# A two-hop graph layer and an adjacency-ranked layer in one kernel: row-end products merged, x and the adjacency laid out anew in memory

## The chip, the cores and the metric

One Trainium2 chip, of which the program uses one core. The metric is the device time of one execution in microseconds, as the median of several runs. Lower is better.

## The reference, cut to what matters

N is 4096 nodes, D is 64 features. `adj` is 4096 x 4096, float32, with about 0.8% non-zeros and a full diagonal.

```
h = relu(layernorm(x))
for k in range(2):                         # layer 0, two hops
    agg = adj @ h
    h = tanh(concat([agg, h]) @ W[k])      # W[k] is 128 x 64
x = x + h
h = relu(layernorm(x))                     # layer 1
support = h @ weight
mask = (adj != 0)
rank = cumsum(mask, axis=1)
deg = rank[:, -1:]
k = min(deg, 100)
pos = rank - (deg - k)
w = mask * where(pos > 0, 0.5 ** (k - pos), 0)
x = x + (w @ support + bias)
```

So the adjacency is needed as numbers twice (two hops), and once as an ordered mask, from which the weights of layer 1 come as powers of two.

## The kernel before, in words

The adjacency is transposed on the host, so that a block is 128 source nodes (on the partitions) by a chunk of 1024 destination nodes. There are 4 chunks ("rows", index I) of 32 blocks; a block is 512 KB.

Sweep 1 reads every block of every row once, two blocks (a "pair", 1 MB) to a load (L396), 64 pairs in all, as far ahead as there is space. A place is either one of three pair-sized slots of `ring`, or a stretch of `codes` that is not yet needed. For each pair, DVE (and for some pairs ACT, L227 and L228) makes the mask and running counts (`count_pair`, L236 to L248), and PE multiplies the features `h` with the block into `acc`. Blocks of nodes whose x1 (the result of hop one) is known already are "fused": the weights hold h and x1 side by side, 128 columns (L438, one matmul of 0.86 us for 512 columns). Others use 64 columns, two matmuls side by side on the halves of the array (L254, 0.43 us each as a pair goes).

At the end of a row comes `finish_row` (L306), a generator of which one step runs after each pair of the following row, so that PE's work lies between the pairs. ACT copies the sums S and, from row 1 on, F out of PSUM; `totals` (L284) makes the total counts; PE forms `po` and ACT takes its tanh as x1 (transposed); PE turns x1 to node layout with the identity (`nodes`, L208, line L212) and forms in `po1` what the known part gives to hop two (L323, L329, and for row 0 L344, with G summed from blocks that were held); ACT copies both out. Then `set_after` (L293) gets, by products with `tri` and `neg`, how many entries lie behind each half of the blocks, in two rounds (v = 1, 0), and `settle` (L366) subtracts that from the codes.

Sweep 2 reads again, one block (512 KB) to a load (L832), the 72 blocks that hop two still lacks: first those of chunks 3 and 2, then 1, then 0. It has six slots of `ring`, four from block 24 on. `finish_last` (L473) is the row end of row 3 and runs between the first blocks. When a chunk's sum is complete, `finish_x2` (L511) finishes x2: it adds the stored part by a product with the identity (L518), multiplies the sum (L531), takes tanh, adds the input x (loaded again as `xres`, L525), and makes LayerNorm and a split into three bf16 parts. That makes the chunk ready for layer 1.

Layer 1 goes by 64 units of two blocks by a destination chunk. A unit's codes are turned to bf16 weights by ACT (L642, L649) or DVE (L624 to L638), PE multiplies them with the high parts (L692) and then the low part (L704), and when a group of four units ends, the sums are taken out of PSUM (L722 to L741). `finish_out` (L746) multiplies with the layer's weight and adds the residual. The units run between sweep 2's blocks; the last 28 or 30 after them.

The order of all of sweep 2 is written by a planner inside the kernel: `use(engine, us, after)` keeps an estimated clock for each engine, `space` says from when a buffer is free, and `run_chain`, `decode` and `fill` place the next step by these clocks. So an edit of a step's estimated duration, or of when a buffer is given to `space`, moves the order of instructions on PE, ACT and DVE. All loads are issued by SP, in program order: an SP instruction that waits for a buffer holds back all loads behind it.

Of the kernel before, what the change touches and what calls it, by code (L numbers as in the profile page):

```python
# [36 lines left out]
def gnn_kernel(  # L37
# [20 lines left out]

    nc = tc.nc

    N, D = x.shape
# [46 lines left out]
    xv = x.rearrange("(p b) d -> p b d", b=NB)  # L108
# [14 lines left out]
    def load_x(engine, b0, b1):  # L123
        engine.dma_start(pre1[:, b0:b1, :], xv[:, b0:b1, :])
# [7 lines left out]

    def load_weights():
        for h in range(2):
            rows = slice(h * D, (h + 1) * D)
            nc.sync.dma_start(wz[rows, h], Wd)
            nc.sync.dma_start(wa[rows], weight)
            nc.gpsimd.tensor_copy(wh[rows, h], wa[rows])

# [10 lines left out]
    ident = cpool.tile([P, P], F32, name="ident")  # L150
# [4 lines left out]
    neg = cpool.tile([P, P], BF16, name="neg")  # L155
    nc.vector.tensor_scalar(neg, diff, 0.0, -1.0, op0=ALU.is_equal, op1=ALU.mult)

    off = cpool.tile([P, 2], F32, name="off")
    for h in range(2):
        nc.vector.tensor_scalar(  # L160
            off[:, h : h + 1], diff[:, P - 1 : P], float(2 * FULL), float((1 - h) * FULL),
            op0=ALU.mult, op1=ALU.add,
        )
# [43 lines left out]

    def nodes(src):  # L208

        pt = one(name="pt")  # L210
        for t in range(TC):
            nc.tensor.matmul(  # L212
                pt[:, t * P : (t + 1) * P], by_t(src)[:, t // 2, t % 2, :], ident,
                start=True, stop=True, skip_group_check=True,
            )
        return pt.rearrange("p (t c e) -> p t c e", t=TC, c=NC)
# [67 lines left out]
    def totals(I):  # L284

        both = tmp([P, CW], U8, name="both")
        nc.vector.tensor_tensor(both.bitcast(U16), cnts[I % 2][0], cnts[I % 2][1], op=ALU.add)  # L287
        tot = [tmp([P, CW], BF16, name="tot") for _ in range(2)]
        nc.scalar.copy(tot[0], both)  # L289
        nc.scalar.copy(tot[1], cnts[I % 2][1].bitcast(U8))  # L290
        return tot

    def set_after(I, v, tot, banks):  # L293

        for c, pb in enumerate(banks):
            nc.tensor.matmul(  # L296
                pb, tri if v else neg, tot[1 - v][:, c * C : (c + 1) * C],
                start=v == 1, stop=True, skip_group_check=True,
            )
        for c, pb in enumerate(banks):  # L300
            nc.vector.tensor_scalar(  # L301
                after[:, v, I * CW + c * C : I * CW + (c + 1) * C], pb,
                off[:, v : v + 1], float(K), op0=ALU.add, op1=ALU.min,
            )

    def finish_row(I, acc, held):  # L306
        S = tmp(name="S")
        nc.scalar.copy(S, acc[:, NC, :])
        if I:
            F = [tmp(name="F") for _ in range(NC)]  # L310
            for c in range(NC):
                nc.scalar.copy(F[c], acc[:, c, :])
        tot = totals(I)
        yield
        po = one(name="po")
        terms = [(lambda c: wz[:, c, 0, 0], lambda c: S)]
        if I:
            terms.append((lambda c: wz[:, 0, 0, 0], lambda c: F[c]))
        x1T = x1_of(po, I, terms)
        po1 = two(name="po1")  # L320
        if I:
            for c in range(NC):
                nc.tensor.matmul(  # L323
                    po1[c * D : (c + 1) * D, :], wz[:, 1, 1, 0], F[c], start=True, stop=False
                )
        yield
        pt = nodes(x1T)
        for c in range(NC):
            nc.tensor.matmul(  # L329
                po1[c * D : (c + 1) * D, :], wz[:, c, 1, 1], x1T, start=I == 0, stop=I > 0  # L330
            )
        nc.scalar.copy(as_nodes(hx[:, chunk(I), D:]), pt)
        yield
        if I == 0:

            own = [v for k in sorted(held) for v in held[k]]
            for n, (b, a) in enumerate(own):
                agg_pair(acc[:, 0, :], hx[:, b, D:], a, n == 0, n == len(own) - 1)
            held.clear()
            G = tmp(name="G")  # L340
            nc.scalar.copy(G, acc[:, 0, :])
            yield
            for c in range(NC):
                nc.tensor.matmul(  # L344
                    po1[c * D : (c + 1) * D, :], wz[:, c, 1, 0], G, start=False, stop=True
                )
        nc.scalar.copy(flat(pre1[:, chunk(I), :]), po1)
        yield
        banks = [one(name="pb"), two(name="pb")]
        for v in (1, 0):  # L350
            set_after(I, v, tot, banks)
            yield
        all_settle(I)
# [16 lines left out]
    def sweep1():  # L370
        b0 = NB - 2
        load_x(nc.sync, b0, NB)
        load_x(nc.sync, NB - CB, b0)
# [5 lines left out]
        def load(upto, done):  # L379

            while len(tiles) < min(upto, len(pairs)):
# [10 lines left out]
                if k == 0:  # L392
                    for r in range(2):
                        nc.sync.dma_start(a[:, r, :], adjA[I, n + r])
                else:
                    nc.sync.dma_start(a, adjA[I, n : n + 2].rearrange("r p i -> p r i"))  # L396
# [3 lines left out]
        for k, (I, b) in enumerate(pairs):  # L400
# [3 lines left out]
            if k == 0:  # L404
                load(1, 0)
                load_x(nc.sync, NB - 2 * CB, NB - CB)
                load(2, 0)
                load_x(nc.sync, 0, NB - 2 * CB)
# [54 lines left out]
        return acc, totals(I)  # L463
# [9 lines left out]
    def finish_last(acc, tot):  # L473

        I = NCH - 1
        S = tmp(name="S")
# [4 lines left out]
        use("ACT", 1.7, 0.2)  # L481
# [7 lines left out]
        pt = nodes(x1T)  # L489
        nc.scalar.copy(as_nodes(hx[:, chunk(I), D:]), pt)  # L490
        use("ACT", 0.6, use("PE", 1.3) + 0.2)
        po1 = two(name="po1")
        for c in range(NC):
            nc.tensor.matmul(
                po1[c * D : (c + 1) * D, :], wz[:, 1, 1, 0], F[c], start=True, stop=False
            )
        for c in range(NC):
            nc.tensor.matmul(
                po1[c * D : (c + 1) * D, :], wz[:, c, 1, 1], x1T, start=False, stop=True
            )  # L500
        nc.scalar.copy(flat(pre1[:, chunk(I), :]), po1)
        use("ACT", 0.6, use("PE", 1.9) + 0.2)
        yield
        banks = [one(name="pb"), two(name="pb")]
        for v in (1, 0):
            set_after(I, v, tot, banks)
            use("DVE", 1.4, use("PE", 0.5) + 0.2)
            yield
        all_settle(I)

    def finish_x2(I, acc):  # L511

        h = chunk(I)

        pt = one(name="py")
        v = by_t(flat(pre1[:, h, :]))
        for t in range(TC):
            nc.tensor.matmul(  # L518
                pt[:, t * P : (t + 1) * P], v[:, t // 2, t % 2, :], ident,
                start=t == 0, stop=False, skip_group_check=True,  # L520
            )
# [3 lines left out]
        nc.sync.dma_start(xres, xv[:, h, :])  # L525
        t0 = use("ACT", 0.6, clock["PE"] + 0.2)
        use("PE", 1.25)
        yield t0 + 0.1
        v = by_t(S)
        for t in range(TC):  # L530
# [3 lines left out]
                start=False, stop=True, skip_group_check=True,  # L534
            )
        y = tmp(name="y")
        nc.scalar.activation(y, pt, AF.Tanh)
        yield use("ACT", 0.65, use("PE", 1.25) + 0.2) - 0.5
        nc.vector.tensor_tensor(
            as_nodes(pre1[:, h, :]), as_nodes(xres), y.rearrange("p (t c e) -> p t c e", t=TC, c=NC),  # L540
            op=ALU.add,
        )
        t = use("DVE", 0.7, clock["ACT"] + 0.1)
# [132 lines left out]
    def layer1(n):  # L676
# [20 lines left out]
        use("PE", 0.2)  # L697
        for i, acc in zip(todo, accs):
# [10 lines left out]
        for i, acc in zip(todo, accs):  # L709
# [12 lines left out]
            if g not in parted:  # L722
                parted.add(g)
                for q, p in enumerate(part(g)):
                    (nc.vector.tensor_copy if q == 1 else nc.scalar.copy)(p, acc[:, q, :])
                    use("DVE" if q == 1 else "ACT", 0.65, t)
            elif J:
                for q, p in enumerate(part(g)):
                    nc.vector.tensor_tensor(p, acc[:, q, :], p, op=ALU.add)
                    use("DVE", 0.65, t)  # L730
            else:
                ys = part(g)
                for q, p in enumerate(ys):
                    nc.vector.tensor_tensor(p, acc[:, q, :], p, op=ALU.add)
                t = use("DVE", 1.9, t)
# [7 lines left out]

    outs = []

    def finish_out(g, ys):  # L746
        last = g == order[0][-1]
        pt = (one if g % 2 else two)(name="pto")
# [3 lines left out]
        for ks in [range(K4)] if not last else [range(K4 // 2), range(K4 // 2, K4)]:  # L752
            for k in ks:
                cols = slice(k * P, (k + 1) * P)
                for c in range(NC):
                    nc.tensor.matmul(  # L756
                        pt[:, k * P + c * D : k * P + (c + 1) * D], ys[c][:, cols], wa,
                        start=k == c == 0, stop=not last, skip_group_check=True,
# [12 lines left out]
    def sweep2(acc, tot):  # L771
# [7 lines left out]
        space(quad(mbuf.rearrange("p a r i -> p (a r i)").bitcast(I16)))  # L779
# [5 lines left out]
        last = finish_last(acc, tot)  # L785
# [33 lines left out]
        for n in range(0, total, 2):  # L819
# [8 lines left out]
            for r in range(2):  # L828
# [3 lines left out]
                nc.sync.dma_start(a, adjA[I, NB - 1 - b - r])  # L832
# [45 lines left out]
    sweep2(*sweep1())  # L878
# [26 lines left out]
```

## Time and profile before

| what | us |
|---|---|
| median of 3 runs | 392.31 (390.9 to 392.37) |
| the profiled execution | 390.78 |
| its span | 389.0 |
| PE busy | 365.5 (94%) |
| DVE busy | 301.4 (77%) |
| ACT busy | 166.2 (43%) |
| sweep 1's last product ends on PE | 205.5 |
| last adjacency block of sweep 2 used | 333.3 |

Busy time of PE is the time with at least one matmul in flight; matmuls are pipelined, so the mean duration of one (0.6 us for L254) is longer than what it adds to the row. What a matmul costs when they follow closely is read from the chain: four matmuls of L254 with their weight loads ("x8") take 1.72 us there. PE was granted its full clock but for a stretch near 14 to 21 us.

The loads move 108.5 MB. All are made of packets of at most 4 KB: in the trace's packet records 25,728 of 4096 bytes (median 159 ns), 1024 of 2048 bytes (81 ns at the fastest), and a few smaller. At full use the core gets some 410 GB/s.

### The profile page before, as it was taken

Reading aid. Unit: us, or ns where it says so; the run is one execution under the profiler, and the core shown is the slowest. Engines: PE = TensorE matmul, PEld = TensorE weight load, DVE = VectorE, ACT = ScalarE, POOL = GpSimd, SP = SyncE. Lnnn points to the kernel's source line nnn. Section 1 sums busy time; section 2 is a strip of 40 time slices with the busy share of each in tenths; the row PEclk is TensorE's granted clock in tenths of the full one; section 3 lists DMA queues with packets and bytes.
Section 4 is the critical chain, followed back from the end, with each engine's and each line's share of the span. In section 5 each row is a group of like instructions: output and inputs, shape, how many; then the busy total and the mean of one; then the engine's idle time right before and its main releaser. Section 6 shows DMA issues by size and latency. Waiting matters only on the chain.

```text
span 389.0 us, 4496 instructions
## 1 busy us (share of the span) xinstructions
PE 365.5 (94%) x1654; PEld 144.5 (37%) x1668; DVE 301.4 (77%) x565; ACT 166.2 (43%) x164; POOL 22.7 (6%) x21
## 2 busy tenths in 40 slices
PE   3698789999999999999999988999999999999995
PEld 0142223234333443444443323333343333434554
DVE  5979989499989999699889697777846844389943
ACT  2179980754363433410004111744246945388200
POOL 2202100000000000000000030300003000030000
PEclk9699999999999999999999999999999999999999
DMA  7999999999997896578999799588876887000011
GB/s 229 415 411 406 365 408 407 409 408 409 410 345 270 313 327 235 205 291 305 293 350 317 250 417 401 182 283 305 304 265 224 313 312 258 2 2 2 0 56 54
DMA packets 30150, 108.50 MB, mean 279 GB/s; under 512 B 2736, under 2 KB 3376, under 8 KB 30128
## 3 DMA queue, kind: packets, MB, share of 16 engines
q1 hardware_dynamic: 30128, 108.21, 75.0%
q8 instruction: 13, 0.21, 0.2%
q14 instruction: 9, 0.07, 0.1%
HBM read 107.15 MB, written 1.05 MB: 278 GB/s over the span
## 4 chain that ended last, share of the span: by engine, by line
PE 79%; DMA 13%; SPq 3%; ACT 2%; issue 1%; DVE 0%; ACTq 0%
PE acc L254 25%; PE acc L438 21%; PE accl L692 15%; PE accl L704 8%; DMA codes<-in_adjA_dram 8%; DMA ring<-in_adjA_dram 5%; SPq L396 3%; PE po L196 2%; PE pto L756 2%; PE pt L212 1%; ACT codes L227 1%; PE pb L296 1%; PE py L518 1%; ACT codes L228 1%; PE po L329 1%
## 5 line engine op out<-in xcount | busy, mean ns | idle before, releaser
L254 PE MATMUL acc<-ring,hx 128*64 128x512 f32 x384 | 95.6, 623 | 12.2 <-DVE hx L186 6.4
L438 PE MATMUL acc<-ring,hx 128*128 128x512 f32 x152 | 66.2, 593 | 0.0
L254 PE MATMUL acc<-codes,hx 128*64 128x512 f32 x256 | 59.3, 598 | 5.5 <-DMA codes<-in_adjA_dram 5.5
L254 PEld LDWEIGHTS acc<-ring,hx 128*64 128x64 f32 x384 | 25.6, 140 | 66.3 <-issue 31.6
L438 PEld LDWEIGHTS acc<-ring,hx 128*128 128x128 f32 x152 | 28.8, 190 | 36.0 <-issue 35.7
L248 DVE TENSOR_SCALAR lo<-codes 128x512 uint16<-128x512 uint16 x128 | 37.6, 294 | 4.4
L247 DVE TENSOR_TENSOR codes<-mbuf,lo 128x512 uint16<-128x512 uint16 x90 | 38.3, 425 | 3.1
L692 PEld LDWEIGHTS <-hx 128*128 128x128 bf16 x256 | 23.2, 98 | 39.7 <-issue 12.6
L366 DVE TENSOR_TENSOR codes<-codes,after 128x2048 uint16<-128x2048 uint16 x32 | 37.6, 1217 | 0.0
L183 POOL TENSOR_TENSOR s<-s,half 128x8 f32<-128x8 f32 (+2 forms) x9 | 16.7, 1852 | 323.1 <-DVE s L182 323.1
L236 DVE TENSOR_SCALAR mbuf<-ring 128x2048 uint8<-128x2048 f32 x27 | 32.9, 1220 | 2.0 <-DMA ring<-in_adjA_dram 2.0
L228 ACT ACTIVATE codes<-codes 128x1024 uint8<-128x1024 int8 x32 | 33.8, 1057 | 1.0
L254 PEld LDWEIGHTS acc<-codes,hx 128*64 128x64 f32 x256 | 17.7, 138 | 43.3 <-issue 30.5
L227 ACT ACTIVATE codes<-codes 128x1024 int8<-128x1024 f32 x24 | 25.1, 1047 | 16.1 <-DMA codes<-in_adjA_dram 16.1
L642 ACT ACTIVATE codes<-codes,zero 128x2048 int16<-128x2048 uint8 x14 | 27.2, 1992 | 9.7 <-PE accl L704 9.7
L692 PE MATMUL accl<-codes,hx 128*128 128x512 bf16 x118 | 29.2, 380 | 0.2
L642 ACT ACTIVATE ring<-codes,zero 128x2048 int16<-128x2048 uint8 x11 | 21.7, 1995 | 11.0 <-PE accl L704 11.0
L236 DVE TENSOR_SCALAR mbuf<-codes 128x2048 uint8<-128x2048 f32 x21 | 25.6, 1219 | 0.0
L301 DVE TENSOR_SCALAR after<-pb,off 128x512 uint8<-128x512 f32 x16 | 11.4, 745 | 13.3 <-PE pb L296 13.3
L289 ACT CAST tot<-both 128x1024 bf16<-128x1024 uint8 x4 | 4.2, 1057 | 37.7 <-DVE both L287 37.7
L692 PE MATMUL accl<-ring,hx 128*128 128x512 bf16 x74 | 18.8, 380 | 0.6 <-issue 0.2
L704 PEld LDWEIGHTS <-lo 128*64 128x64 bf16 x256 | 12.2, 109 | 19.0 <-issue 10.6
(109 smaller groups left out, 354.8 us busy)
## 6 DMA issues: line engine op xcount, KB each, us to landing
ring<-in_adjA_dram SPq DMA_DIRECT2D x74, 512.0 KB, 5.0
codes<-in_adjA_dram SPq DMA_DIRECT2D x33, 1024.0 KB, 12.5
ring<-in_adjA_dram SPq DMA_DIRECT2D x30, 1024.0 KB, 5.6
xres<-in_x_dram SPq DMA_DIRECT2D x4, 256.0 KB, 5.9
out_dram<-o SPq DMA_DIRECT2D x3, 256.0 KB, 2.5
pre<-in_x_dram SPq DMA_DIRECT2D x1, 512.0 KB, 9.8
pre<-in_x_dram SPq DMA_DIRECT2D x1, 256.0 KB, 6.8
out_dram<-o SPq DMA_DIRECT2D x2, 128.0 KB, 1.9
```

Source lines behind the costliest of these rows:

```text
L183: nc.gpsimd.tensor_tensor(s2, s2, half[:, :nb], op=ALU.pow)
L227: nc.scalar.activation(sign, a[:, r], AF.Sign)
L228: nc.scalar.activation(m, sign, AF.Square, scale=float((FLAG - 1 + 0.25) ** 0.5))
L236: nc.vector.tensor_scalar(m, a, 0.0, float(FLAG - 1), op0=ALU.not_equal, op1=ALU.mult)
L247: nc.vector.tensor_tensor(q, marks[r].bitcast(U16), cnt, op=ALU.add)
L248: nc.vector.tensor_scalar(cnt, q, 0x7F7F, None, op0=ALU.bitwise_and)
L254: nc.tensor.matmul(acc[c * D : (c + 1) * D, :], src, a[:, c * C : (c + 1) * C], start=first, stop=last,)
L366: nc.vector.tensor_tensor(q, q, a[:, None, :].to_broadcast([P, 4, CW // 2]), op=ALU.subtract)
L438: nc.tensor.matmul(acc[:, c, :], hx[:, g, :], a[:, r, c * C : (c + 1) * C], start=g == CB * I - 1, stop=g == 0,)
L642: nc.scalar.activation(w.rearrange("p r k x y -> p r k (x y)"), src.rearrange("p r (y k) -> p r k y", k=2), AF.Relu, scale=float(FLAG), bi ...
L692: nc.tensor.matmul(like(accs[-1][:, c, :], w), hm[:, CB * J + 2 * k + r, : 2 * D], w[:, r, c], start=first and r == 0, stop=last and r == 1,)
L704: nc.tensor.matmul(like(acc[c * D : (c + 1) * D, 2, :], w), lo[:, CB * J + 2 * k + r, :], w[:, r, c], start=first and r == 0, stop=last an ...
```

## The change

Layout. On the host, the adjacency goes from `(4, 32, 128, 1024)` to `(4, 16, 128, 2, 1024)`: the two blocks of a pair lie side by side, so that a load of sweep 1 reads one run of 8 KB for each partition, and a load of one block in sweep 2 reads runs of 4 KB that lie 8 KB apart. x goes from rows in order to four chunks of `128 x (8 x 64)`, each contiguous, and is loaded in four chunks (256 KB), as is `xres`.

```diff
-                    nc.sync.dma_start(a, adjA[I, n : n + 2].rearrange("r p i -> p r i"))
+                    nc.sync.dma_start(a, adjA[I, n // 2])
...
-                nc.sync.dma_start(a, adjA[I, NB - 1 - b - r])
+                nc.sync.dma_start(a, adjA[I, (NB - 1 - b - r) // 2, :, (NB - 1 - b - r) % 2])
...
-    def load_x(engine, b0, b1):
-        engine.dma_start(pre1[:, b0:b1, :], xv[:, b0:b1, :])
+    def load_x(q):
+        nc.sync.dma_start(pre1[:, chunk(q), :], x[q])
...
-        load_x(nc.sync, b0, NB)
-        load_x(nc.sync, NB - CB, b0)
+        load_x(NCH - 1)
...
                 load(1, 0)
-                load_x(nc.sync, NB - 2 * CB, NB - CB)
+                load_x(2)
                 load(2, 0)
-                load_x(nc.sync, 0, NB - 2 * CB)
+                load_x(1)
+                load(3, 0)
+                load_x(0)
```

Row ends. x1 is turned to node layout and multiplied for hop two in one product: the moving operand `both_w` holds the identity and the second hop's weights side by side (256 columns), and the result lies in two PSUM banks in node layout. For rows 1 and 2 the two sums that use the same weights are copied on top of each other (T), and the other halves go to Fx.

```diff
+    def x1_and_share(I, x1T, Fx):
+        banks = [one(name="pt"), two(name="pt")]
+        v = by_t(x1T)
+        for h, pt in enumerate(banks):
+            pt = pt.rearrange("p (t w q) -> p t w q", t=2, w=2)
+            if Fx is not None:
+                f = by_t(Fx)
+                for t in range(2):
+                    nc.tensor.matmul(
+                        pt[:, t, 1, :].rearrange("p (c e) -> p c e", c=NC), f[:, h, t, :], wz[:, :, 1, 0, :],
+                        start=t == 0, stop=False, skip_group_check=True,
+                    )
+            for t in range(2):
+                nc.tensor.matmul(
+                    pt[:, t, :, :], v[:, h, t, :], both_w,
+                    start=Fx is None and t == 0, stop=True, skip_group_check=True,
+                )
+        return banks
+    def take(dst, banks, w):
+        for h, pt in halves_of(banks, w):
+            nc.scalar.copy(as_nodes(dst)[:, 2 * h : 2 * h + 2], pt)
...
         if I:
-            F = [tmp(name="F") for _ in range(NC)]
+            T = [tmp(name="T") for _ in range(NC)]
             for c in range(NC):
-                nc.scalar.copy(F[c], acc[:, c, :])
+                nc.scalar.copy(T[c][:D], acc[:D, c, :])
+                nc.scalar.copy(T[c][D:], acc[c * D : (c + 1) * D, NC, :])
+            Fx = tmp(name="Fx")
+            for c in range(NC):
+                nc.scalar.copy(Fx[c * D : (c + 1) * D], acc[D:, c, :])
+            terms = [(lambda c: w0, lambda c: T[c])]
```

The counts behind a half. `set_after` multiplies once, with `tri`; the earlier half's number is made from it on DVE. `totals` casts one total instead of two, and for row 3 works in `mbuf`.

```diff
+        early = after[:, 0, cols]
+        nc.vector.tensor_scalar(
+            early.bitcast(U16), cnts[I % 2][1], -1.0, float(FULL * 257), op0=ALU.mult, op1=ALU.add
+        )
+        nc.vector.tensor_tensor(
+            early.bitcast(U16), early.bitcast(U16), after[:, 1, cols].bitcast(U16), op=ALU.add
+        )
+        nc.vector.tensor_scalar(early, early, float(K), None, op0=ALU.min)
```

Hop two's end. The stored part is in node layout now, so it is added by DVE after the product, and the product with the identity goes.

```diff
-        for t in range(TC):
-            nc.tensor.matmul(
-                pt[:, t * P : (t + 1) * P], v[:, t // 2, t % 2, :], ident,
-                start=t == 0, stop=False, skip_group_check=True,
-            )
...
-        y = tmp(name="y")
-        nc.scalar.activation(y, pt, AF.Tanh)
+        nc.vector.tensor_tensor(
+            as_nodes(y), pt.rearrange("p (t c e) -> p t c e", t=TC, c=NC), as_nodes(pre1[:, h, :]),
+            op=ALU.add,
+        )
+        nc.scalar.activation(y, y, AF.Tanh)
...
+        nc.vector.tensor_add(pre1[:, h, :], xres, y)
```

Layer 1. The first two of a group's three sums are taken out (`evict`) before the low-part products, the third after them; new sums all go by ACT. The last output uses two PSUM banks for its two halves.

```diff
+        for i, acc in zip(todo, accs):
+            J, g, k = units[i]
+            if k == CB // 2 - 1 and (J, g) not in kept:
+                evict(J, g, acc, (0, 1))
...
+            t = evict(J, g, acc, (2,))
...
-        pt = (one if g % 2 else two)(name="pto")
...
         for ks in [range(K4)] if not last else [range(K4 // 2), range(K4 // 2, K4)]:
+            pt = (one if (g + bool(ks.start)) % 2 else two)(name="pto")
```

The planner's numbers for the changed steps change with them, and `mbuf` is given to `space` after row 3's end instead of at the start of sweep 2. By the order of the instructions, PE has in sweep 2 one pair of blocks more before the first `py` product, two layer-1 units before the second and the fourth, and one pair of blocks before the third.

## The prediction
> **What bounds the kernel now.** I read the page's busy slices first, then the chain of work that ended last in order of time, then windows of the stretches where that chain changes hands, then the timelines of DVE and ACT near the end.
>
> ```profile
> PE   3698789999999999999999988999999999999995
> GB/s 229 415 411 406 365 408 407 409 408 409 410 345 270 313 327 235 205 291 305 293 350 317 250 417 401 182 283 305 304 265 224 313 312 258 2 2 2 0 56 54
> PE 79%; DMA 13%; SPq 3%; ACT 2%; issue 1%; DVE 0%; ACTq 0%
> ```
>
> A slice is 9.7 us. The first five are at 365 to 415 GB/s with PE below full (the opening one only 229); from slice six on PE is full, with one dip in slices 24 and 25, where the loads are at 401 to 417 again. So DMA sets the time of row 0 and of a piece near 225 to 240 us; PE sets the rest. What is taken from PE elsewhere counts in full, unless something else is late next.
>
> ```profile
> 39.02 11.73 DMA codes<-in_adjA_dram
> 50.78 1.07 ACT codes L227
> ...
> 54.87 0.58 ACT S L308
> ...
> 104.19 2.58 PE po L196 x12
> 106.77 0.86 PE po L323 x4
> 107.63 1.72 PE acc L254 x8
> 109.34 1.14 PE pt L212 x8
> 110.48 1.01 PE po L329 x4
> ...
> 232.14 6.53 DMA ring<-in_adjA_dram
> 239.79 1.14 PE py L518 x8
> 240.93 0.94 PE py L531 x8
> ```
>
> Columns: start, us, work. Row 0's last pair lands at 50.78, ACT marks it, then S is copied and PE goes on. The middle is the end of row 1; an "x" counts weight loads too, so "x12" is six matmuls. The last three lines close the second DMA stretch.
>
> ```profile
> 7.00:8.00 1.00, 1.00 (x4) 0.18 (x2) 0.44 (x2) 0.00 (x0) 0.44 (x1) 1.00 0.79 162
> 10.00:11.00 1.00, 0.00 (x0) 0.00 (x0) 0.96 (x3) 0.07 (x1) 0.00 (x0) 1.00 1.06 434
> 220.00:222.00 2.00, 2.00 (x13) 0.59 (x10) 2.00 (x4) 0.00 (x0) 0.00 (x0) 1.00 0.74 127
> 238.00:240.00 2.00, 1.80 (x10) 0.48 (x7) 2.00 (x3) 0.11 (x1) 0.00 (x0) 1.00 1.04 410
> ```
>
> The last column is GB/s. Summing the windows from 2 us on in queue order, the x chunk of 2 KB runs (8 KB apart) falls at 7 to 8, at 162; the x load of 4 KB runs, also 8 KB apart, at 10.6 to 11.9, at 410 to 434. In sweep 2 the first xres (2 KB runs) falls at 220 to 222, at 127; the second, at 237.5 to 239.5, at full rate. So 2 KB strided runs are sometimes slow, and 4 KB ones were not.
>
> **The change part by part.** The sum is made against the profiled execution, 390.78 us, 389.0 of it span. E is the end of sweep 1 on PE (205.5), T the end of its last x1 block (333.3).
>
> *Start, x by chunks.* Against 410 GB/s, the one-us windows from 3 to 9 us (185, 365, 393, 348, 162, 330) miss 677 KB, that is 1.65 us. x now comes in contiguous chunks. Bounds 0 (contiguous x as slow) and -1.65; I take -1.5. The first chunk is 256 KB where 64 KB came: it lands some 0.4 us later (3.15), but the second LayerNorm part no longer waits until 4.98, so the first product stays near 6.3. DVE follows too: its 1.28 us wait at 21.5 was for ACT marks of a pair that comes earlier.
>
> *8 KB runs.* The trace's packet records have 159 ns for 4 KB, 81 for 2 KB: 3 ns per packet and the rest by size, so 8 KB should take 315 against 318, 1% of the 41 us of row 0's loads: -0.4. Nearest 8 KB rows are instruction fetches, 310 at best and 342 in the median: bounds -1.0 and +3.0. A rule says more: the Trainium skill, Perfetto Trace Analysis, "DMA Optimizations", holds that going to 4 or 8 KB can raise throughput dramatically. With the fabric ceiling of 435 GB/s of "DMA: Bandwidth & Descriptors", "Specifications", that is an estimate of -2.4 us here and a sum near 380; the packet records speak for less.
>
> *Ends of rows 1 and 2.* Before: po 2.58, L323 0.86, pt 1.14, L329 1.01, two pairs of pb 1.08: 6.67. After: po four matmuls 1.72; four Fx products of 128 columns at L212's rate 1.14; four products of 256 columns at half of L438's 0.86, 1.72; one pb pair 0.54: 5.12. Against it ACT makes T in four half-height copies (a copy follows the last by 0.5) where po began after one: T[1] is ready at 104.5, PE wants it at 104.05; two matmuls run side by side, so I take +0.3 (0 to 0.5). -1.25 each, -2.5. Fx and its copies run while PE has the next pair (1.72). Behind them on ACT stand tot and the tanh: 102.36 + 6 x 0.5 + 1.05 + 0.6 = 107.0, before PE asks at 107.9.
>
> *End of row 0.* pt, L329, L344 (3.01) become 1.8 + 1.0, and 0.54 of pb goes: -0.75. Both banks now leave by ACT copies behind 4.2 us of marks, where 0.68 of idle stood before: +0.4. -0.35.
>
> *set_after on DVE.* Two of L301's 0.745 go; a 16-bit scalar op (L248, 0.29), an add (L247, 0.43) and a byte op of 1024 elements, for which no row stands (0.29 by L248, 1.22 by L236), come. -0.8 to +0.5; only settles follow, and DVE has slack from 77% busy. Nothing. POOL's three new copies (0.28 each by L138) come after its last LayerNorm and are wanted 10 us later: nothing.
>
> *Head of sweep 2.* Six slots: block n's load goes out when block n-6 is used. PE's work at the row end falls from 6.67 to 2.58 + 1.14 + 1.72 + 0.54 = 5.98; block 4 is used at E+9.75 (1.72 + 2.58 + 1.72 + 2.86 + 0.86), so block 10 can land at E+13.1 (3.3 is the shortest from issue to landing). From there the queue is full: block 11, xres (0.65 at full rate), blocks 12 to 23 at 1.28: E+30.4; PE starts 0.67 later and takes 0.86: E+31.9 (was 34.26). Then a layer-1 pair 2.82 and py 0.98, without L518: E+35.7, where E+39.05 stood: -3.35. With xres at 127 GB/s it is -1.3. x2's chain has a DVE add and two blocks more ahead; its last op comes at about E+31.7, when PE asks.
>
> *Half rows.* Sweep 2 now reads 4 KB runs 8 KB apart. The window at 10 us says no cost: 0. The other side is the rival below. The same DMA page ("Latency and other measured facts") warns of power-of-two row pitches halving the rate; its smallest is 512 KiB and no run here shows it at 8 KB. By it (an estimate) the sum would be some 430.
>
> *Chunk 1.* L518 goes, -1.14; S now hides under one pair of blocks (1.72).
>
> *Chunk 0.* L518 goes as well, but py stands behind a layer-1 pair, and the chain to x2 starts 1.65 later. From T, by the rows: py 3.75, add 4.7, tanh 5.4, two conversions of 1.4 on DVE, residual and LayerNorm to 9.6, square 10.3; then ACT has five conversions (1.95 each) before it casts hx: 20.6; subtract and cast on DVE: 21.9. PE could start the last 16 units at T+20.7; it starts near 22.0. It was 21.66. +0.35 (-0.9 with no wait, +3 if the conversions wait themselves).
>
> *Tail.* The last out in two banks frees PE of the 0.52 it waited at 383.92: -0.5. Earlier evictions hide behind products: nothing, PE was not waiting.
>
> Sum: -1.5 -0.4 -2.5 -0.35 -3.35 -1.14 +0.35 -0.5 = -9.4: 381.4. The median, 392.31, stands 1.5 above the profiled execution (runs 390.9 to 392.37), which would make 382.9; I say **382.0**.
>
> **The rivals.**
> *x stays slow* (the two slow spells were the address, not the stride), and 8 KB brings nothing: gives back 1.5 + 0.4 + 2.05: 386. For it: the xres at 238 was as strided and not slow. Against: 4 KB runs and all contiguous loads were never slow. 0.17.
> *Chain of chunk 0 late*: DVE or ACT order makes PE wait 4 to 5 us at the last units instead of 1.3: 385.5. For it: the residual add stood 4 us behind accumulator adds before (y ready at 336.06, add at 339.99); against: the first three of those adds now start earlier. 0.12.
> *Half-row loads slow, slower than before*: PE uses a block per 1.85 us (88.7 us for the last 48), so up to that the price is only on some 13 DMA-bound blocks. At 250 GB/s (2.1 us) it is 13 x 0.82 + 48 x 0.25 = 22.7: 404. It decides from 1.9 us a block (276 GB/s): 13 x 0.62 + 48 x 0.05 = 10.5 outweighs the 9.4. For it: the x rows at 127 and 162; against: 434 for 4 KB runs. 0.08.
> *It doesn't do what it says*: packets stay at 4 KB; costs the 0.4: 382.4, inside the forecast.
>
> **How the numbers follow.** The forecast has 0.63, with its own 379 to 384.5. The range 378.5 to 387.5 takes in the two milder rivals and leaves out the slow loads and a little on both ends. A difference under 0.5% (about 2 us) can't be told from none here. Faster 0.88; same 0.04 (two mild rivals together, and an 8 KB packet at 342); slower 0.08.
>
> **What would show it.** Right: row 0's last pair landing at 48.5 to 49, E near 200.7, no 127 GB/s window in sweep 2, block 24's stretch from 236, no L518's. T some 9.2 earlier, a wait of about 1.3 of PE before the last 16 units, on the cast of hx. Wrong: packets of 8 KB over 320 ns, sweep-2 windows under 400 GB/s while PE waits for ring, or PE idle in rows 1 to 3, which would mean that DVE's slack is not there.

## The result, and the profile after

The changed kernel takes **413.4 us** (median of 4 runs, 411.43 to 417.52) against 392.34 before (390.9 to 392.89): 1.056 times as long, 95% interval 1.046 to 1.065. It is slower, where 382.0 was predicted. The profiled execution took 411.86 us, 409.8 of it span, at a mean clock of 0.99. Here and below a median is of all executions and a ratio of the fast ones alone, which leaves out those over 1.5% above the fastest of the same kernel (two of ten in `e1`, three of ten in `e2`, one of six in `e12`).

The page of the changed kernel, three rows of its 40 slices (10.2 us each here):

```profile
PE   3788899999999999999997886889988899698876
PEclk9999999999999999999999996999999999999999
GB/s 272 427 420 387 416 417 421 421 420 421 318 233 368 327 254 139 352 301 308 325 283 351 409 227 105 255 276 255 235 224 266 248 252 146 1 2 0 27 26 51
```

The transfers did as predicted. Slices 2 to 10 are at 416 to 427 GB/s where 406 to 415 stood (one exception in each), and the first at 272 instead of 229. But PE, which before was at 80% or more in every slice from six on but the last, has many digits of 6 to 8 from slice 22 on. The list of PE's waits in the same trace, its nine longest (engine, its line, what it waited for: us in total, times, longest), says for whom:

```profile
PE accl L715 <- DVE codes L753: 11.9, 8, 2.3
PE acc L245 <- DMA ring<-in_adjA_dram: 7.4, 15, 2.0
PE accl L715 <- ACT codes L750: 6.9, 4, 3.4
PE acc L245 <- DVE hx L187: 6.4, 1, 6.4
PE acc L245 <- DMA codes<-in_adjA_dram: 4.4, 8, 0.9
PE acc L245 <- DVE codes L238: 1.5, 1, 1.5
PE acc L245 <- ACT S L527: 0.9, 1, 0.9
PE accl L698 <- DVE hx L566: 0.7, 1, 0.7
PE accl L698 <- ACT mbuf L648: 0.5, 1, 0.5
```

L715 is the third product of layer 1; L750 and L753 are the copies and adds of the new `evict`. These two lines, 12 waits and 18.8 us, weren't there before. One of them, in the timelines of PE and of DVE (start, us, engine, line, operation; in brackets the idle time before it and what ended it):

```profile
373.13 1.03 PE L698 MATMUL accl<-codes,hx 128*128 128x512 bf16 x4
375.54 1.49 PE L715 MATMUL accl<-ring,lo 128*64 128x512 bf16 x12 [1.38 <-DVE codes L753]
```

```profile
374.19 1.29 DVE L753 TENSOR_TENSOR codes<-accl,codes 128x512 f32<-128x512 f32 x2 [0.83 <-PE accl L698]
377.49 0.69 DVE L753 TENSOR_TENSOR codes<-accl,codes 128x512 f32<-128x512 f32 x1 [2.01 <-PE accl L715]
```

PE ends L698 at 374.16. DVE then adds `acc[:, 0]` and `acc[:, 1]` until 375.48, and only then does L715 start, though it writes `acc[:, 2]`, which nobody reads yet. After it DVE adds the third sum. The three are one PSUM tile, and the two engines take turns. Before, the third product (L704) followed the first two (L692) at once, and DVE made its three adds in a row behind it, here for two neighbouring groups:

```profile
377.21 1.03 PE L692 MATMUL accl<-codes,hx 128*128 128x512 bf16 x4
378.17 0.62 PE L704 MATMUL accl<-codes,lo 128*64 128x512 bf16 x4
```

```profile
372.90 1.89 DVE L734 TENSOR_TENSOR codes<-accl,codes 128x512 f32<-128x512 f32 x3 [3.11 <-PE accl L704]
```

Where the rest went shows in four points of the time line. E is the first sweep-2 product, T the end of the last x1 block, the last column the end of PE's last product. The first three rows are from the two traces and the prediction's sum; the two below belong to experiments told further down.

| kernel (profiled execution, us) | E | block 24 starts | T | PE ends |
|---|---|---|---|---|
| before | 205.53 | 244.41 | 333.31 | 385.53 |
| as predicted | 200.8 | 236.3 | 324.1 | 376.1 |
| after | 202.30 | 241.50 | 346.05 | 406.33 |
| late eviction, pairs | 201.61 | 241.42 | 334.50 | 386.41 |
| two PSUM tiles, old layout | 203.29 | 240.95 | 331.18 | 382.66 |

Three things went wrong, then: E came 3.2 earlier instead of 4.75, the head of sweep 2 gave nothing instead of 3.35, and from block 24 on the kernel lost 23.7 us (164.8 against 141.1), of which 18.8 are the waits above and up to 3.4 a spell of half clock (last section).

### The profile page after: what moved, and what is told of

Its sections match the earlier page's. It is cut to its first block, busy times and chain, and to the rows that moved or that the text cites. A ratio compares the mean times of both kernels' runs of the same rounds, so it can differ in the third digit from the quotient of the medians.

```text
span 409.8 us, 4423 instructions
## 1 busy us (share of the span) xinstructions
PE 364.2 (89%) x1606; PEld 147.2 (36%) x1620; DVE 302.7 (74%) x573; ACT 167.5 (41%) x176; POOL 24.9 (6%) x24
## 3 DMA queue, kind: packets, MB, share of 16 engines
HBM read 107.15 MB, written 1.05 MB: 264 GB/s over the span
## 4 chain that ended last, share of the span: by engine, by line
issue 47%; PE 29%; DMA 14%; DVE 5%; ACT 2%; POOL 1%; SPq 0%; POOLq 0%; ACTq 0%
PE accl L698 11%; PE acc L245 8%; PE accl L715 7%; DMA ring<-in_adjA_dram 4%; DMA codes<-in_adjA_dram 4%; DMA wa<-in_weight_dram 4%; DVE codes L753 3%; PE pto L771 2%; DMA pre<-in_x_dram 2%; ACT ring L648 1%; ACT codes L750 1%; PE py L535 1%; POOL s L184 1%; DVE xc L187 0%; DVE s L178 0%
## 5 line engine op out<-in xcount | busy, mean ns | idle before, releaser
L245 PE MATMUL acc<-ring,hx 128*64 128x512 f32 x384 | 98.3, 631 | 14.8 <-DMA ring<-in_adjA_dram 7.4
L245 PE MATMUL acc<-codes,hx 128*64 128x512 f32 x256 | 60.3, 598 | 5.9 <-DMA codes<-in_adjA_dram 4.4
L245 PEld LDWEIGHTS acc<-ring,hx 128*64 128x64 f32 x384 | 27.2, 143 | 71.1 <-issue 31.6
L698 PEld LDWEIGHTS <-hx 128*128 128x128 bf16 x256 | 23.2, 98 | 41.7 <-issue 15.7
L753 DVE TENSOR_TENSOR codes<-accl,codes 128x512 f32<-128x512 f32 x24 | 15.8, 687 | 28.4 <-PE accl L698 15.8
L245 PEld LDWEIGHTS acc<-codes,hx 128*64 128x64 f32 x256 | 17.6, 136 | 41.6 <-issue 27.7
L698 PE MATMUL accl<-codes,hx 128*128 128x512 bf16 x115 | 28.8, 380 | 0.5 <-issue 0.2
L648 ACT ACTIVATE codes<-codes,zero 128x2048 int16<-128x2048 uint8 x13 | 25.3, 1991 | 8.8 <-PE accl L715 8.8
L648 ACT ACTIVATE ring<-codes,zero 128x2048 int16<-128x2048 uint8 x10 | 20.0, 1996 | 20.6 <-PE accl L715 14.9
L715 PEld LDWEIGHTS <-lo 128*64 128x64 bf16 x256 | 14.6, 110 | 36.8 <-issue 30.2
L715 PE MATMUL accl<-codes,lo 128*64 128x512 bf16 x124 | 16.8, 383 | 9.2 <-DVE codes L753 9.2
L698 PE MATMUL accl<-ring,hx 128*128 128x512 bf16 x77 | 19.3, 380 | 0.3
## 6 DMA issues: line engine op xcount, KB each, us to landing
wz<-in_Wd_dram SPq DMA_DIRECT2D x2, 64.0 KB, 16.2
```

The costliest lines, as they stand in the source:

```text
L245: nc.tensor.matmul(acc[c * D : (c + 1) * D, :], src, a[:, c * C : (c + 1) * C], start=first, stop=last,)
L648: nc.scalar.activation(w.rearrange("p r k x y -> p r k (x y)"), src.rearrange("p r (y k) -> p r k y", k=2), AF.Relu, scale=float(FLAG), bi ...
L698: nc.tensor.matmul(like(accs[-1][:, c, :], w), hm[:, CB * J + 2 * k + r, : 2 * D], w[:, r, c], start=first and r == 0, stop=last and r == 1,)
L715: nc.tensor.matmul(like(acc[c * D : (c + 1) * D, 2, :], w), lo[:, CB * J + 2 * k + r, :], w[:, r, c], start=first and r == 0, stop=last an ...
```

## The experiments

In each group the kernel before ran on the same chip; its medians were 392.4 to 393.3.

| run | median us | ratio to before, 95% |
|---|---|---|
| late eviction, pairs (`e1`) | 394.82 | 1.003 (0.999 to 1.007) |
| two PSUM tiles, pairs (`e2`) | 393.88 | 1.001 (0.997 to 1.005) |
| after, old layout (`e3`) | 409.97 | 1.044 (1.039 to 1.049) |
| before, early eviction (`e4`) | 412.13 | 1.051 (1.045 to 1.057) |
| late eviction, old layout (`e5`) | 389.09 | 0.989 (0.985 to 0.992) |
| two PSUM tiles, old layout (`e6`) | 388.46 | 0.988 (0.986 to 0.991) |
| before, pairs (`e7`) | 395.87 | 1.006 (1.003 to 1.010) |
| as e5, six slots longer (`e8`) | 393.28 | 1.001 (0.998 to 1.004) |
| as e6, no Fx share in the last row end (`e9`) | 387.17 | 0.986 (0.981 to 0.991) |
| as e6, two x loads left out (`e10`) | 387.60 | 0.986 (0.981 to 0.991) |
| as e2, whole pairs in sweep 2 (`e11`) | 392.37 | 1.001 (0.998 to 1.004) |
| as e6, far pairs (`e12`) | 397.06 | 1.007 (1.005 to 1.010) |

**Is it the early eviction?** Take it out of the changed kernel, and put it alone into the kernel before:

```diff
--- e1, against after
-        for i, acc in zip(todo, accs):
-            J, g, k = units[i]
-            if k == CB // 2 - 1 and (J, g) not in kept:
-                evict(J, g, acc, (0, 1))
...
-            t = evict(J, g, acc, (2,))
+            t = evict(J, g, acc, (0, 1, 2))
--- e4, against before: the opposite, with the changed kernel's evict()
```

> The changed kernel, but with all three sums of a unit evicted after the unit's L715 products, as the kernel before does; everything else of the change stays. Theory A (the early eviction makes TensorE wait in front of L715: 12 waits, 18.8 us in the profile after, and the idle time brings a clock of 0.5 for 6.8 us, some 3 us more): the 12 waits of L715 are gone, and the time is 384 to 393 us. Rival B (the waits only stand where TensorE would have waited anyway, for half rows, new row ends or a late cast): other waits take their place, and the time stays at 403 to 413.

> The kernel before with one thing of the change alone: the first two sums of a unit are evicted between its L698 products and its L715 products (there with other line numbers). Theory A: TensorE waits 1.2 to 1.4 us for each of 12 evictions, 14 to 19 us in sum, time 404 to 412. Rival B: 391 to 394, the eviction is free as predicted and the loss needs the other parts.

Without it 394.82, 18.6 us less than the changed kernel; alone in the kernel before, 412.13. PE's waits in e4 (there L708 is the third product, L743 and L746 the eviction):

```profile
PE accl L708 <- DVE codes L746: 11.9, 8, 2.1
...
PE accl L708 <- ACT codes L743: 5.7, 4, 2.2
```

Eight and four waits again, 17.6 us for a loss of 19.3 (412.13 less 392.82). In e1 no wait on L711, the third product there, is left. So theory A holds by removal and by addition. The sizes agree less closely than 17.6 and 19.3 look: the profiled execution of e4, at a clock of 0.999, took 409.0, 16.2 above that median; the other three, 410.88 to 413.5, had mean clocks of 0.989 to 0.993. And e1 is 1.8 us above the range given: the rest of the change, worth all of the 9.4 in the prediction, brings nothing that can be told from zero here.

**Is it a clash in PSUM, or the tile?**

```diff
--- e2, against after
-    sums[g] = pacc.tile([P, 3, C], F32, tag="acc", name="accl")
+    class Acc: a = pacc.tile([P, 2, C], F32, tag="acc"); l = pacc.tile([P, C], F32, tag="accs")
...
-    like(acc[c * D : (c + 1) * D, 2, :], w), lo[...]
+    like(acc.l[c * D : (c + 1) * D, :], w), lo[...]
```

> The changed kernel with its early eviction, but the sums in PSUM lie in two tiles: the two of L698 in one, the one of L715 in another, in the same banks as before. Theory A1 (L715 waits only because it writes another part of a tile that the eviction still reads; there is no shared address): no wait of L715 for L750 or L753, time 383 to 392, at or a little under the late eviction. Rival A2 (the reads and the products really meet in PSUM, or a new tile of the second kind comes free late): L715 still waits 1.2 to 1.4 us for each eviction, time 405 to 413.

393.88, not to be told from e1's 394.82: the early eviction costs nothing any more, with the sums in two tiles and as many PSUM bytes. The same place in e6, which has the same two tiles (L723 is now the third product, L761 the add), in the timelines of PE and of DVE:

```profile
375.12 1.03 PE L706 MATMUL accl<-codes,hx 128*128 128x512 bf16 x4
376.08 0.62 PE L723 MATMUL accls<-codes,lo 128*64 128x512 bf16 x4
376.53 1.03 PE L723 MATMUL accls<-ring,lo 128*64 128x512 bf16 x8
377.40 0.60 PE L723 MATMUL accls<-codes,lo 128*64 128x512 bf16 x4
```

```profile
376.19 1.29 DVE L761 TENSOR_TENSOR codes<-accl,codes 128x512 f32<-128x512 f32 x2 [2.52 <-PE accl L706]
378.04 0.69 DVE L761 TENSOR_TENSOR codes<-accls,codes 128x512 f32<-128x512 f32 x1 [0.56 <-PE accls L723]
```

DVE's adds (376.19 to 377.48) and PE's products (376.08 to 378.0) run at the same time, and neither is slower for it: 681 ns for an add where the taking of turns had 691, 379 ns for a product in both. The wait was ordering by tile, not a limit of PSUM. What the early eviction brings once it is free is some 0.4 us from T to PE's end (51.48 in e6, 51.88 in e5), in one trace of each.

**Is the layout to blame?** The layout of before (4 KB of one block after another) goes into the changed kernel, into e1 and into e2; and the pairs go alone into the kernel before.

```diff
--- e3 against after, e5 against e1, e6 against e2 (e7 against before: the reverse)
-    nc.sync.dma_start(a, adjA[I, n // 2])
+    nc.sync.dma_start(a, adjA[I, n : n + 2].rearrange("r p i -> p r i"))
-    nc.sync.dma_start(a, adjA[I, (NB - 1 - b - r) // 2, :, (NB - 1 - b - r) % 2])
+    nc.sync.dma_start(a, adjA[I, NB - 1 - b - r])
```

> The changed kernel with its early eviction, but adjacency in the layout of before (one block after another, 4 KB runs per partition in sweep 1, and 512 KB in one piece for every block of sweep 2). Theory A (the layout is worth what its packets say, 309 against 2 x 159 ns, and the loss lies in the eviction): 411 to 415, the 12 waits of L715 unchanged. Rival C (half rows of the new layout make sweep 2 slow): 385 to 398.

> The changed kernel with all three sums evicted after L715 (as in the run with the late eviction) and with adjacency in the layout of before. What is left of the change: x by chunks, the merged row ends, the new ends of the chunks in sweep 2. Theory D (half of a pair, 4 KB out of every 8 KB, lands later in sweep 2: the median landing in sweep 2 was 5.9 us with the pairs and 4.8 with the old layout under the early eviction; with four slots in the ring every microsecond of it is a wait): median landing near 5, the DMA waits of blocks 24 to 71 (3.2 us with the pairs, the S wait in it) fall to about 1, time 386.5 to 391, under the late eviction with pairs. Rival E (the landing time differs for another reason, the pairs cost nothing): 392 to 396, as with the pairs.

> As the run before this one, but with the early eviction and the sums in two PSUM tiles. Theory: the early eviction is then off TensorE's path and shortens only the last evictions after J = 0: 0 to 1 us under the late eviction with the old layout, 386 to 391. If the two kinds of tile cost a wait of their own, it is above it by 1 or more.

> The kernel before with the layout in pairs alone: 8 KB runs per partition in sweep 1, half of a pair per load in sweep 2. Theory D: sweep 1 ends 0 to 1 us earlier, but sweep 2's loads land later (5.1 us median before, about 6 then) and the four-slot ring has no slack for it: 393.5 to 398. Rival E, and the prediction's own term (-0.4): 391.5 to 393.

e3, under the early eviction, came out a little under its range (409.97), a hint against the pairs, though its interval and the changed kernel's overlap. With the eviction out of the way they cost 5.7 us by the medians (394.82 less 389.09) and 5.4 (393.88 less 388.46), 5.7 and 5.0 by the ratios; alone in the kernel before 3.4, or 2.4 by the ratio. The two profiled executions show less: PE ends 2.4 us later in e1 than in e5 (386.41, 384.03). Part of the rest goes with the clock: the four executions of e1 with a mean clock under 0.992 are its four longest, 396.5 to 398.8, where all six of e5 had 0.998 or more. Sweep 1 does gain: E is 1.3 us earlier with the pairs (201.61, 202.91 in e5), more than the 0.4 predicted. Sweep 2 pays more. The list of transfers from 205 us on, first for e1 and then for e5 (queue, times, KB each, median us from issue to landing):

```profile
ring<-in_adjA_dram SPq DMA_DIRECT2D x64, 512.0 KB, 5.9
```

```profile
ring<-in_adjA_dram SPq DMA_DIRECT2D x65, 512.0 KB, 5.3
```

With four slots a block's load goes out when the block four places before it is used. Where a layer-1 pair lies in between, before and e5 have 5.18 us from issue to use, with no wait (block 34: 253.83 to 259.01 in e5). It had landed 4.0 us after issue. In e1 the same load went out at 254.05, landed after 6.36 and PE got it at 260.45, after an idle 1.05. Of the 48 blocks from 24 on, 18 take longer than 5.18 us to land in e5 and 31 in e1; PE's waits before them are 1.6 and 3.2 us.

**The pitch, or two halves in flight together?** In e12 blocks n and n + 16 share the 8 KB runs: no load gets a run of 8 KB, and the two halves of a run are never asked for side by side.

```diff
--- e12, against e6
-    nc.sync.dma_start(a, adjA[I, NB - 1 - b - r])
+    nc.sync.dma_start(a, adjA[I, (NB - 1 - b - r) % 16, :, (NB - 1 - b - r) // 16])
```

> As the run with two PSUM tiles and the old layout (388.5 us), but blocks n and n + 16 of a slab share the 8 KB runs, so every load takes 4 KB out of every 8 KB, in sweep 1 (two blocks a load) and in sweep 2 (one), and the other half of a run is never loaded beside it. Theory K (the pitch: 4 KB at 8 KB lands later than 4 KB at 4 KB, whatever else is in flight): sweep 2's median landing near 5.9 us instead of 5.0, time 391 to 396. Theory L (the two halves of one run in flight together hurt each other): landing near 5.0, time 388 to 390.

397.06, 8.6 us above e6 (7.5 by the two ratios): theory K, the pitch by itself, and at a higher price than expected. The profiled execution (399.78) has two spells of half clock, worth up to 3.4 us of it, which belong to the price only in so far as the waits bring them (last section); but the two executions at a clock of 0.999 took 394.8 and 395.48, still 6 to 7 above e6. Its median landing is 5.7 us against 5.0 in e6. In sweep 1 the same pitch costs nothing: E at 203.0, 203.3 in e6, and 404 GB/s from 15 to 95 us in both, with 165 ns for the mean packet in both. The loads there queue behind one another. From 245 to 330 us, where one or two stand alone, the mean packet of 4 KB takes 199 ns against 185, and 14% of them against 8% take over 250 ns; the median is 159 in both. So it is a tail of late packets in lone loads, and no lower rate. Why they come late no run here shows.

**Can 8 KB runs serve both sweeps?**

```diff
--- e11, against e2: one load of a whole pair into two neighbouring slots
+    nc.sync.dma_start(ring[:, pair[0] : pair[0] + 2, :], adjA[I, (NB - 1 - b) // 2])
```

> The changed kernel with two PSUM tiles and adjacency in pairs, but sweep 2 loads a whole pair at once, 1 MB in 8 KB runs into two neighbouring slots, not two halves of 4 KB runs. The packets are then never half of a run. Theory I (8 KB runs help both sweeps once no half is taken, 309 ns against 2 x 159): 386 to 390, below the same kernel with half rows (393.9). Rival J (a pair needs both its slots free and lands only when all of 1 MB has come: four slots are then two buffers, and TensorE waits 1 us or more for most pairs of sweep 2): 400 to 425.

392.37: neither theory's range, and not to be told from e2's 393.88. The pairs land steadily, most within 4.6 to 5.3 us, but PE waits 10.4 us for ring loads, 4.9 in e6. That a whole pair goes out later than its first half could have is a likely reason; it wasn't isolated.

**More slots for longer** (e5 with `if n == 40` for `if n == 24`):

> As the late eviction with the old layout, but the ring keeps its six slots until block 40 of sweep 2 instead of block 24; two slots of decoded codes come later for that. Theory F (the loads of sweep 2 wait for a slot: a block's load goes out when the block four places ahead is done): the waits on ring loads between blocks 24 and 40 go, up to 1 us, unless layer 1 then waits for decoded codes; 386 to 392. If decoding needs the space: waits of L698 for ring or codes, 393 or more.

393.28, 4.2 above e5: the space was needed. L698 waited 2.0 us for decoded codes in `hx` and 0.6 for those in `mbuf`, which e5's list of waits doesn't have.

**What sets the head of sweep 2?**

```diff
--- e9, against e6
-        banks = x1_and_share(I, x1T, Fx)
+        banks = x1_and_share(I, x1T, None)
--- e10, against e6: no xres for chunks 3 and 2, y added to itself
-        nc.vector.tensor_add(pre1[:, h, :], xres, y)
+        nc.vector.tensor_add(pre1[:, h, :], y if xres is None else xres, y)
```

> As the run with two PSUM tiles and the old layout (388.5 us), but the last chunk's row end leaves out its share of Fx: eight 128x128 products (0.74 and 0.62 us in the head of sweep 2), so pre1 of chunk 3 lacks that term. Theory G (the head of sweep 2 is set by the ring: six slots, and from block 10 on a load every 1.28 us, where TensorE waits for each): what TensorE saves there turns into more waiting on ring loads, blocks 17 to 23 start within 0.5 us of where they did relative to the end of sweep 1's last slot, and the time stays within 0.5 us, 387.5 to 389. Rival H (TensorE sets the head, as the prediction counted): 1.2 to 1.4 us less, 386.8 to 387.3.

> As the run with two PSUM tiles and the old layout (388.5 us), but the x residual of chunks 3 and 2 isn't loaded again in sweep 2 (y is added twice in its place): two transfers of 256 KB less, 0.64 us each at 409 GB/s, no product less. Theory G (the transfers set the head): blocks 17 to 23 come about 0.6 us earlier, block 24 some 0.6 to 1.3 us earlier, time 387 to 388. Rival H (TensorE sets the head): no change of the head, 388 to 389.

The times, 387.17 and 387.60, can't be told apart from each other or, by their intervals, from e6. The traces give no verdict either. From E to the issue of block 24's load (which waits for the slot of block 18) it takes 26.73 in e6. Without one 256 KB transfer on the way it takes 26.09, 0.64 less; without the Fx products, which let block 10's load go out 0.94 earlier (9.21 after E, 10.15 in e6), it takes 26.21, 0.52 less. But e5, whose program is the same up to there except for the tiles, takes 27.35: single traces differ by 0.6 where nothing was taken away. How the loads pace PE is seen in PE's timeline of e1:

```profile
217.51 1.08 PE L245 MATMUL acc<-ring,hx 128*64 128x512 f32 x4 [0.82 <-DMA ring<-in_adjA_dram]
218.78 1.08 PE L245 MATMUL acc<-ring,hx 128*64 128x512 f32 x4 [0.19 <-DMA ring<-in_adjA_dram]
221.80 2.24 PE L245 MATMUL acc<-ring,hx 128*64 128x512 f32 x8 [1.94 <-DMA ring<-in_adjA_dram]
...
234.48 1.08 PE L245 MATMUL acc<-ring,hx 128*64 128x512 f32 x4 [0.21 <-DMA ring<-in_adjA_dram]
235.75 1.08 PE L245 MATMUL acc<-ring,hx 128*64 128x512 f32 x4 [0.19 <-DMA ring<-in_adjA_dram]
```

Each "x4" is a block. Block 10 starts at 217.51, as soon as its load, out at 211.76, has landed (217.47, 5.7 us). Before, it went out at 215.67, landed at 219.01, 3.3 later, and PE came for it at 221.12, without any wait. The layout decides here: block 10 lands after 3.3 to 4.5 us in all traces with the old layout and after 5.1 to 5.7 in those that load halves of a pair. Blocks 22 and 23 stand 1.27 us apart, each behind a wait, the pace of 512 KB at 409 GB/s. Less work of PE alone can't shorten that part; before had the same pace from block 14 on.

## Why the prediction was wrong

**The step that failed** is the last, "Earlier evictions hide behind products: nothing, PE was not waiting." It asked what an eviction behind L698 takes from ACT and DVE, not who must wait for it: the next writer of the same PSUM tile is L715, on PE itself. PE's 12 waits, up to 3.4 us long, are 18.8 of the 31 us by which the prediction missed; e1, e2 and e4 show that it is the early eviction, and by way of the shared tile. None of its rivals had it.

**Half rows, at 0** and the rival at 404: the rival asked for a lower rate, and the rate held at 409 GB/s in the window from 220 to 240 us. What changed was the time to land, for which four slots leave little room: 5.0 to 5.7 us for the layout as a whole, after its gain in sweep 1. The window at 10 us, which was read as "no cost", was of queued loads. The Trainium skill, DMA: Bandwidth & Descriptors, "Latency and other measured facts", has pitches of 4 MiB and more halve the rate; at 8 KB e12 shows the full 404 GB/s, and a loss all the same.

**8 KB runs, at -0.4**: the packet was right (309 ns in the median here, 315 predicted), but E's gain between e5 and e1 is 1.3. The sum took the median of 4 KB packets, 159; in the queue of sweep 1, from 15 to 95 us, the mean is 165.6 in e5 and 316 for 8 KB in e1, 5% less for the same bytes instead of 1%. The dramatic gain that the Trainium skill, Perfetto Trace Analysis, "DMA Optimizations", names, with 2 KB to 4 or 8 KB as its example, is not in these runs, which go from 4 to 8 KB.

**Head of sweep 2, at -3.35**: -1.2 in e6, -0.6 in e5, and +0.9 in e1. The order was right, block 10 behind the slot of block 4. Its load went out at E+10.15, as before (10.13), not at 9.75. With the old layout it landed about as counted (3.36 us after issue in e5, 4.5 in e6; 3.3 counted), but the queue was not full from there: block 11 landed at E+16.5 in e5 and E+15.9 in e6, where 14.4 was counted. With the pairs block 10 itself took 5.7 (e1). The 0.67 counted between block 23's landing and PE's start is 0.05 in the traces. So block 23 starts at E+32.6 in e5; 31.1 was counted, and before it was 33.2. Then PE waits for x2 of chunk 3, whose last op was put at E+31.7, "when PE asks"; PE got it at E+34.3. PE's timeline of e5:

```profile
235.53 1.08 PE L245 MATMUL acc<-ring,hx 128*64 128x512 f32 x4 [0.19 <-DMA ring<-in_adjA_dram]
237.26 1.02 PE L698 MATMUL accl<-hx 128*128 128x512 bf16 x4 [0.65 <-DVE hx L566]
```

**Ends of rows 1 and 2, at -1.25 each**: -0.72 and -0.13. In PE's timeline of the changed kernel, at the end of row 1, and in ACT's:

```profile
101.65 1.40 PE L197 MATMUL po<-T,w 128*64 128x512 f32 x3
102.51 0.59 PE L197 MATMUL po<-pre,wz 128*64 128x512 f32 x1
102.89 0.59 PE L197 MATMUL po<-T,w 128*64 128x512 f32 x1
```

```profile
100.58 0.58 ACT L333 COPY T<-acc 64x512 f32<-64x512 f32 x1
101.18 0.58 ACT L332 COPY T<-acc 64x512 f32<-64x512 f32 x1
101.77 0.59 ACT L333 COPY T<-acc 64x512 f32<-64x512 f32 x1
```

The copies follow each other by 0.6, not 0.5, and the last ends at 102.36, when PE has been at `po` for 0.7 us. The stretch of `po` took 2.6 us in row 2 (149.43 to 153.76 with a pair of 1.72 in it), where 1.72 + 0.3 was counted. And the steps that were replaced took 6.4 us in row 2 before (152.53 to 155.97, 157.78 to 159.83 and two pairs of `pb` of 0.44), not 6.67. The rest wasn't isolated.

**Chunk 1, at -1.14**: L518 went, but "S now hides under one pair of blocks" fell. PE's timeline of e1:

```profile
285.77 1.88 PE L245 MATMUL acc<-ring,hx 128*64 128x512 f32 x8
288.56 1.94 PE L245 MATMUL acc<-ring,hx 128*64 128x512 f32 x8 [0.91 <-ACT S L527]
290.43 1.21 PE L535 MATMUL py<-wz,S 128*128 128x128 f32 x8
```

It isn't `py` that waits for S, but the next chunk's first block. The L518 products had covered the copy; 0.91 of the 1.14 came back as a wait.

**What was right:** the start (the last pair of row 0 starts 1.63 earlier, -1.9 predicted with the 8 KB), the end of row 0 (-0.75, -0.35 predicted), `set_after` and POOL at nothing, and the way through T to the end once the eviction is out (-0.3 in e1 and e5, -0.15 predicted), with the wait of PE for the cast of `hx` before the last 16 units (1.15 in e5, 1.3 predicted). The rival that x stays slow fell: the first `xres` took 186 ns for the mean packet of 2 KB before and 85 after (107 in e1, 106 in e5).

**The sum.** Of 31.4 us between prediction and result, 18.6 are the eviction (413.4 less 394.82) and 5.7 the layout (394.82 less 389.09), where -0.4 was counted (some of either came by way of the low clock). The other 7 or so are the gains that did not come: head 2.8, row ends and E 1.7, and from block 24 to T some 3 (0.9 for S, 0.5 for a late `mbuf`, 0.5 at ring loads; the cause of the rest stays open), by the milestones of e5. The best version found is e6: the change without the layout in pairs and with the sums in two tiles, 388.46 us, 0.988 of before (0.986 to 0.991).

## What to carry to other kernels

Before an eviction or any read is moved ahead of a product, look who writes the same tile next: an engine that waited for nothing will then wait for the reader; here two tiles cured it. Where a ring of few slots has its round trip (issue, landing, use) just covered by compute, a layout is to be judged by how late a lone load lands, not only by the rate of queued ones; where the loads already set the pace, work taken from PE turns into waiting. A copy that is "hidden" is hidden by particular instructions; when they go, it isn't.

## What the runs showed of the hardware

- VectorE read two parts of an accumulator's banks while TensorE wrote the third, and neither slowed: 681 ns for an add, 379 for a product.
- 4 KB runs at a pitch of 8 KB kept the full rate when loads queued (404 GB/s), but raised the mean packet of lone loads from 185 to 199 ns and their landing from 5.0 to 5.7 us.
- An f32 product stands in PE's rows as two records, a bf16 one as one: L254 has 640 records for the 320 products of 160 blocks. The "x8" of the chain before is four products by these, not by their weight loads; the costs read from it are the same.
- The changed kernel's profiled execution had a spell of half clock in its longest wait, of 3.4 us (245.99 to 249.37). A table of windows of it, and then one of e2's (from:to, us, then busy time of PE, PEld, DVE, ACT and POOL with instructions, clock, DMA share, GB/s):

```profile
244.40:247.80 3.40, 1.12 (x5) 0.39 (x4) 2.74 (x5) 2.47 (x3) 0.00 (x0) 1.00 0.79 249
247.80:254.60 6.80, 5.23 (x18) 2.22 (x19) 3.65 (x9) 2.10 (x4) 0.34 (x1) 0.50 0.07 27
```

```profile
218.50:221.90 3.40, 1.08 (x4) 0.20 (x5) 0.82 (x1) 0.58 (x1) 0.00 (x0) 1.00 0.98 348
221.90:225.30 3.40, 3.38 (x8) 0.79 (x8) 0.00 (x0) 0.00 (x0) 0.00 (x0) 0.51 1.02 418
```

At 0.5 for 6.8 us the first costs up to 3.4. The traces show eight such spells between 10 us and the tail, in six kernels, each 3.41 or 6.83 us long. Cut each of these six traces into steps of 3.41 us that begin with its spell: in the eight steps just ahead of a spell PE is busy for 32 to 45%, and in no other of some 640 for less than 46%. So in these traces the low clock follows PE's busy share in a fixed step, not the length of one wait. That fits e1 and e4, where waits of 1.9 and 2.2 us brought none in the profiled execution, and it would let executions of one kernel differ by how the steps fall; no run varied that alone.
